# The order of VectorE's queue in a two-layer cross-attention kernel: c and values behind p5, exps, shares and denominators at other stops

## The chip, the cores and the metric

The kernel runs on one core of one Trainium2 chip. The metric is the device time of one execution in microseconds (us); lower is better. A core has five engines with a queue each: TensorE (PE in the profile, its weight loads PEld), VectorE (DVE), ScalarE (ACT), GpSimd (POOL) and SyncE (SP), which here only issues DMAs.

## The reference, cut to what matters

Two cross-attention layers, one behind the other. x is 4 x 512 x 320 (batch, rows, channels), the context 4 x 1024 x 512; 20 heads of 16 channels. The last four context tokens of layer 0 are "image" tokens with weights of their own; in layer 1 the text has 77 tokens and all others are image tokens.

```python
# layer 0
probs_t  = softmax(q @ k_t.T * 0.25)              # 1020 text tokens
text_out = probs_t @ v_t
qsem     = l2norm(probs_t @ text_ehs)             # a 512-wide mix of the raw context, per head
fused    = q @ k_ip.T * 0.25 + 0.5 * (qsem @ ip_n.T)
ip_out   = softmax(fused) * spatial_mask @ v_ip
x        = (text_out + ip_out) @ W_out + b_out + x
# layer 1, on that x
out = (softmax(q @ k.T / 4) @ v + softmax(q @ k_ip.T / 4) @ v_ip) @ Wo.T + bo + x
```

Of qsem only its product with four tokens and its norm are needed. The norm (a sum of squares over 512 columns) makes layer 0 heavy: probs_t times the raw context, for each head.

## The kernel before, in words

**Tiling.** A *turn* is 128 rows of one batch; there are 16. A turn has five *groups* of four heads (80 in all, numbered gi; g is gi modulo 5, turn gi // 5). A group has two *units* (class Unit, i = 0 and 1) of two heads each. The keys lie on partitions, in two halves of four tiles.

**A unit's products.** The matrix product of the two heads' exponentials (four blocks e11, e12, e21, e22; head by half) with the context (two halves of rows, two of columns) is done with seven block products in place of eight, with sums and differences of blocks, as in Strassen's and Winograd's schemes. GpSimd forms the needed combinations of e (L964, L1032, L1051, L1053); sums of the context (t1 to t4) are prepared in DRAM. Text: a product "11·t1" takes block e11 and context block t1. The seven in PE's order, by part:

- part0: b1 = 11·11; ScalarE copies it to p1 (L1050); b2 = 12·21. Then DVE: c = b2 + p1 for the sum of squares of the first head's first half (L1055; ScalarE squares and sums c) and the values of the first head (L1056, 21 columns).
- part1: b3 = 11·t1; DVE copies it to p5 (L1064) and p5's last 21 columns (L1065); then b1 += s2·t2, copied by ScalarE to u (L1068).
- part2: b3 += 12·22, so p5's copy must be done; DVE: c = b3 + u (L1073); b1 += 21·t3; DVE: c = b1 + p5 (L1079, "c of t3").
- part3: b1 += 22·t4, so c of t3 must have been read; ScalarE squares b1, DVE adds the second head's values (L1084).

b1, b2 and b3 are three PSUM banks in rotation. A fourth bank (tp, L105) serves everything else that PE writes in the steady part: transposes of maxima (mx), pt_s, pt_o, pt_y, pt_xT, pt_q, pv and the projections.

**Stops.** After each part comes `stop(gi, k)` (L1262), k = 0 to 3 for the first unit and 4 to 7 for the second. A stop puts one item of other work between the parts:

- scores of the next group in layer 0 (`fill0`, at k = 0 and 2) and of a group of layer 1 (`do_fill`, at k = 4 and 6): 32 short matmuls to `sc`, then per half two maxima on DVE and two copies on ScalarE (L557 to L566);
- folds of these maxima (k = 3, 7, 1), whose transpose on PE (mx) and negated maximum on DVE (zt) follow in part0 or part2; zt goes to DRAM (zd) and comes back broadcast (bc), both issued by SP;
- additions of bc to e, each followed by ScalarE's exp: layer 0's from `ew` (two at k = 6, one at k = 1, one in part2 of the first unit), layer 1's by `do_adds` (one at k = 3, three at k = 5); at k = 6 layer 1's product with its values (pv, 72 instructions);
- items of four lists: `after` and `late` (a finished turn's chain), `norm` (layer 1's denominators, `normalise`, L744: a transpose and a reciprocal on DVE, for even g also a transpose `turn_back`, then two operations on GpSimd, L758 and L759), `proj` (the next batch's projections, while there are any).

**A finished turn's chain.** After a turn's last group `finish` (L1086) runs `norms` at once and queues `exps` (seven small DVE operations, three matmuls pt_s), which queues `shares` (four DVE operations), `turn_out` (transposes pt_o, three copies) and `multiply` (pt_y, an addition to xr); multiply calls `layer1`, which queues x_part (transposes pt_xT), second (pt_q, two writes to q1d) and start (eight loads of layer 1's queries and keys). Layer 1's fifth group brings turn_back and project (pt_y, an addition y, the output's DMA) to the head of `late`.

**What sets the order.** DVE's and PE's instructions are kept in the order in which the program issues them (`vec`, `mm` and `tr`, L77 to L93); DVE instructions thus wait in line behind one that waits. Those of ScalarE, GpSimd and SP are put in order by a planner.

Of the kernel before, what the change touches and what calls it, by code (L numbers as in the profile page):

```python
# [15 lines left out]
ALU = mybir.AluOpType  # L16
# [16 lines left out]
HG = H // 4  # L33
# [12 lines left out]
EH = E // 2  # L46
# [10 lines left out]
def xattn_pair(ctx_stack: ExitStack, tc: tile.TileContext, a: dict, out: bass.AP):  # L57
# [19 lines left out]
    def mm(out, lhsT, rhs, start, stop, on=False):  # L77
        tc.keep_in_program_order(nc.tensor.matmul(out, lhsT=lhsT, rhs=rhs, start=start, stop=stop, skip_group_check=on))  # L78
# [11 lines left out]
    vec = InOrder(nc.vector)  # L90
# [14 lines left out]
    def tp(name):  # L105
        turn_of[0] += 1
        return spare(3 - turn_of[0] % 2 if tail[0] else turn_of[0] % 4 if idle[0] else 3, name)
# [411 lines left out]
    late = deque()  # L519
    proj = deque()  # L520
# [3 lines left out]
    after = deque()  # L524
    ew = deque()
    bits = deque()

    def gap(n=1):
        for _ in range(n):
            if bits:  # L530
                bits.popleft()()
# [74 lines left out]
    class Once:  # L606
# [52 lines left out]
        def ask(self, pt):  # L659

            zd = spread(pt, 8, "zd1", self.name)
            self.bc = bc = big.tile([P, 2, 4, P], F32, tag="bc1", name=f"bc{self.name}")
            keep(nc.sync.dma_start(bc[:NTXT1, 0], zd[0:4, :].partition_broadcast(NTXT1)))
            keep(nc.sync.dma_start(bc[NTXT1:, 0], zd[4:8, :].partition_broadcast(P - NTXT1)))
            keep(nc.sync.dma_start(bc[:, 1], zd[4:8, :].partition_broadcast(P)))
            self.v = load_values(self.z, self.turn, self.g)
# [68 lines left out]
    def do_values():  # L735
        if now["add"] and not now["add"][0].work:
            now["add"].pop(0).values()
# [264 lines left out]
    class Unit:  # L1002
# [43 lines left out]
        def part0(self, between):  # L1046
            self.b1, self.b2 = self.psum(0)[:, 0:WIN], self.psum(1)[:, 0:WIN]
            self.product(self.b1, "11", "11", True)
            self.p1 = big.tile([P, WIN], F32, tag="p1", name=f"p1_{self.name}")
            nc.scalar.copy(self.p1, self.b1)  # L1050
            nc.gpsimd.tensor_tensor(self.e("11"), self.e("11"), self.s2, ALU.add)  # L1051
            self.product(self.b2, "12", "21", True)
            nc.gpsimd.tensor_tensor(self.e("12"), self.e("12"), self.s2, ALU.subtract)  # L1053
            ask = between and between()
            self.add_square(self.b2[:, 0:EH], self.p1[:, 0:EH], 0, 0)  # L1055
            vec.tensor_tensor(self.values(0), self.b2[:, EH:], self.p1[:, EH:], ALU.add)  # L1056
            if ask:
                ask()

        def part1(self):  # L1060
            self.b3 = self.psum(2)[:, 0:WIN]
            self.product(self.b3, "11", "t1", True)
            self.p5 = big.tile([P, WIN], F32, tag="p5", name=f"p5_{self.name}")
            vec.tensor_copy(self.p5[:, 0:EH], self.b3[:, 0:EH])  # L1064
            vec.tensor_tensor(self.p5[:, EH:], self.b3[:, EH:], self.p1[:, EH:], ALU.subtract)  # L1065
            self.product(self.b1[:, 0:EH], "s2", "t2", False)
            self.u = big.tile([P, EH], F32, tag="u", name=f"u_{self.name}")
            nc.scalar.copy(self.u, self.b1[:, 0:EH])  # L1068

        def part2(self, between):  # L1070
            self.product(self.b3[:, 0:EH], "12", "22", False)
            ask = between and between()
            self.add_square(self.b3[:, 0:EH], self.u, 0, 1)  # L1073
            if ask:
                ask()
            if not self.i:
                item(ew)
            self.product(self.b1[:, 0:EH], "21", "t3", False)
            self.add_square(self.b1[:, 0:EH], self.p5[:, 0:EH], 1, 1)  # L1079

        def part3(self):
            self.product(self.b1, "22", "t4", False)
            self.square(self.b1[:, 0:EH], 1, 0)
            vec.tensor_tensor(self.values(1), self.b1[:, EH:], self.p5[:, EH:], ALU.add)  # L1084

    def finish(turn):  # L1086
# [6 lines left out]
        def wide(t, n=NIP):  # L1093
            return t.unsqueeze(2).to_broadcast([P, H, n])
# [30 lines left out]
        def exps():  # L1125
            vec.tensor_tensor(rn, rn, r, ALU.mult)
            vec.tensor_tensor(sem, pv[:, :, D : D + NIP], wide(rn), ALU.mult)
            pt = tp(f"pt_s_{name}")[:, 0 : H * NIP]
            for c in range(NC):
                mm(pt, qt[:, c, :], kd[:, c].rearrange("p h n -> p (h n)"), c == 0, c == NC - 1)  # L1130
            vec.scalar_tensor_tensor(pe, sem, SEM_SCALE, pt.rearrange("p (h n) -> p h n", h=H), ALU.mult, ALU.add)
            vec.tensor_reduce(mx, pe, AX.X, ALU.max)
            vec.tensor_tensor(pe, pe, wide(mx), ALU.subtract)
            nc.scalar.activation(pe, pe, AF.Exp)
            vec.tensor_tensor(o, pv[:, :, 0:D], wide(r, D), ALU.mult)
            gap()
# [31 lines left out]

        def exps_and_on():
            exps()  # L1170
            late.extend([shares, turn_out, multiply])

        (after if turn + 1 < len(TURNS) else late).append(exps_and_on)
# [61 lines left out]
    def item(*queues):  # L1235
        for q in queues:
            if q:
                q.popleft()()
                break

    def visit(gi, k):

        if gi == len(G) - 1:
            if k == 0:
                begin(ep, "e0")
            if k == 4:
                begin(e1p, "e1")
            if k == 6:
                do_values()
                do_adds(2)  # L1250
            do_fill(k // 2 % 2)
            return
        if k < 4:
            fill0(gi + 1, k // 2)
        if k == 4:
            begin(e1p, "e1")
            do_fill(0)
        if k == 6:
            do_values()
            do_fill(1)  # L1260

    def stop(gi, k):  # L1262

        end = gi == len(G) - 1
        if k == 1:
            do_mask() if end else do_rest()
            item(ew)
        if k == 3:
            do_fold(True) if end else fold0(gi + 1)
        if k == 6:  # L1270
            item(ew)
            item(ew)
        if k == 7 and not end:
            do_fold(gi + 1 == len(G) - 1)
        if k == 7 and end and now["fill"]:
            now["fold"] = now["fill"]
            now["fill"] = None
            bits.extend(now["fold"].pieces())
        if k < 3:
            item(after, late, *([proj] if k else []))  # L1280
        elif k % 2:
            item(late, proj)
        do_adds(({3: 4, 7: 2} if end else {3: 1, 5: 3}).get(k, 0))
        if k == 3:
            item(norm)
        if k == 5:
            do_mask()
        if k % 2 == 0:
            visit(gi, k)
        stops[0] += 1  # L1290

    units = {}
# [83 lines left out]
```

## Time and profile before

| | before |
|---|---|
| runs of the kernel, median of 3 | 3320.31 us (3315.03 to 3322.67) |
| the profiled execution | 3314.02 us |
| its span, first to last instruction | 3312.3 us |
| mean granted clock of TensorE | 0.985 |
| steady part, 2127 to 3165 us: busy PE, DVE, ACT, POOL | 1018, 901, 653, 359 of 1038 us |
| last part, 3165 to 3312 us: busy PE, DVE | 117, 86 of 147 us |
| DVE maxima of scores, 128x1024 and 128x768 | 470 x 1222 ns, 150 x 951 ns |
| DVE additions e<-e,bc of 1024 | 470 x 1262 ns |
| a group without projections, turn 13, group 3 | 32.9 us |

A line of a group of instructions reads: line, engine, operation, out<-in, shapes, count, busy time and mean of one, idle time ahead of it and what ended that. A line of waits reads: who waited, for whom, us in total, how often, the longest. A line of the order of time reads: start, duration, instruction, and in brackets idle time ahead with what ended it. All DVE operations of interest have line L88 (a helper), all matmuls L78, so they are told apart by tiles. Consecutive matmuls overlap in the profile: a product of eight matmul instructions takes 1.73 us (256 columns) or 1.87 us (277 columns) from its start to the next one's start, less than the duration shown.

### The profile page before, as it was taken

The page shows a single profiled execution, that of the slowest core. Times are in us where ns is not written, and L with a number is a line of the kernel's source. Part 1 is how long each engine was busy: PE and PEld are TensorE (multiplying, and loading weights), DVE is VectorE, ACT ScalarE, POOL GpSimd, SP SyncE. Part 2 cuts the span into 40 slices and gives each one's busy share as a digit, 9 for nine tenths or more (in the row PEclk, how much of TensorE's full clock was granted, in tenths as well). Part 3 has the DMA queues.
Part 4 walks back from the last instruction along what each step waited for, and adds up shares of the span by engine and source line. Part 5 has one row for each costly group of instructions (what it writes and reads, how often), then busy time and mean ns, then how long its engine had stood idle before and what let it go on. Part 6 is the DMA issues. An engine that isn't in the chain of part 4 may idle for free.

```text
span 3312.3 us, 72573 instructions
## 1 busy us (share of the span) xinstructions
PE 3208.6 (97%) x27740; PEld 2594.7 (78%) x27740; DVE 2506.2 (76%) x4172; ACT 1855.7 (56%) x3373; POOL 1043.7 (32%) x1123
## 2 busy tenths in 40 slices
PE   7999999999999999999999999999999999999988
PEld 5777888878788788887878888887787778787765
DVE  3344577788877777778887787778898888889874
ACT  1333455566555555566655555566666656666643
POOL 3333223323332332323333232323333333333320
PEclk9999999999999999999999999999999999999987
DMA  6433344333444344332344434333233233232221
GB/s 213 112 79 97 96 117 96 92 71 65 102 99 125 92 119 118 75 79 65 68 101 127 121 90 109 97 72 70 58 86 89 63 67 69 59 72 62 64 54 39
DMA packets 648147, 293.89 MB, mean 89 GB/s; under 512 B 491530, under 2 KB 602282, under 8 KB 647802
## 3 DMA queue, kind: packets, MB, share of 16 engines
q1 hardware_dynamic: 646762, 285.65, 36.1%
q8 instruction: 221, 3.62, 0.5%
q0 software_dynamic: 864, 3.41, 0.4%
q14 instruction: 124, 1.02, 0.1%
q10 hardware_dynamic: 176, 0.20, 0.0%
HBM read 248.43 MB, written 40.47 MB: 87 GB/s over the span
## 4 chain that ended last, share of the span: by engine, by line
PE 80%; DVE 10%; DMA 5%; ACT 3%; issue 2%; SPq 1%; POOL 0%; DVEq 0%; POOLq 0%; ACTq 0%
PE b L78 52%; PE sc L78 9%; PE pt_v L78 4%; PE pv L78 4%; PE pt_k L78 4%; DVE e L88 4%; DMA bc<-zd 2%; PE pt_q L78 2%; DVE m L88 2%; PE pt_y L78 2%; DMA zd<-zt 1%; ACT e L561 1%; ACT e L675 1%; DVE x L88 1%; PE mx L78 1%
## 5 line engine op out<-in xcount | busy, mean ns | idle before, releaser
L88 DVE TENSOR_REDUCE m<-sc 128x256 f32<-128x1024 f32 (+1 forms) x620 | 706.9, 1156 | 240.9 <-PE sc L78 166.7
L88 DVE TENSOR_TENSOR e<-e,bc 128x1024 f32<-128x1024 f32 (+2 forms) x770 | 803.5, 1082 | 21.6 <-DMA bc<-zd 21.1
L78 PE MATMUL b<-xv_t,e 128*128 128x277 f32 x2560 | 686.2, 410 | 7.9 <-DVE c L88 7.8
L561 ACT COPY e<-sc 128x1024 f32<-128x1024 f32 x620 | 614.5, 1006 | 82.8 <-DVE m L88 34.2
L78 PE MATMUL b<-xv,e 128*128 128x277 f32 x2560 | 631.3, 398 | 9.2 <-ACT e L962 9.2
L78 PEld LDWEIGHTS b<-xv,e 128*128 128x128 f32 x2560 | 483.4, 190 | 130.6 <-ACT e L962 11.4
L964 POOL TENSOR_TENSOR e<-e 128x512 f32<-128x512 f32 x160 | 230.6, 1441 | 1114.0 <-ACT e L962 1114.0
L78 PEld LDWEIGHTS b<-xv_t,e 128*128 128x128 f32 x2560 | 460.7, 190 | 134.8 <-DVE c L88 11.8
L962 ACT ACTIVATE e<-e 128x1024 f32<-128x1024 f32 x320 | 338.5, 1058 | 225.4 <-DVE e L88 224.6
L675 ACT ACTIVATE e<-e 128x1024 f32<-128x1024 f32 x300 | 316.1, 1058 | 194.3 <-DVE e L88 185.8
L78 PEld LDWEIGHTS sc<-qq,kq 17*128 17x128 f32 (+1 forms) x9920 | 307.1, 186 | 89.9 <-issue 85.0
L78 PE MATMUL sc<-qq,kq 17*128 17x128 f32 (+1 forms) x9920 | 366.8, 283 | 2.1 <-DMA kq<-kd 1.5
L1036 ACT ACTIVATE junk<-c 128x256 f32<-128x256 f32 x480 | 197.6, 412 | 287.8 <-DVE c L88 281.0
L78 PE MATMUL b<-xs,e 128*128 128x256 f32 x1280 | 313.5, 389 | 36.2 <-DVE p L88 27.5
L1051 POOL TENSOR_TENSOR e<-e,s 128x512 f32<-128x512 f32 x160 | 208.4, 1302 | 420.1 <-PE b L78 419.4
L78 PE MATMUL b<-xs_t,e 128*128 128x256 f32 x1280 | 307.3, 384 | 0.0
L78 PEld LDWEIGHTS b<-xs,e 128*128 128x128 f32 x1280 | 241.6, 193 | 81.1 <-issue 47.1
L78 PE MATMUL b<-xs_t,s 128*128 128x256 f32 x1280 | 302.3, 379 | 0.0
L88 DVE TENSOR_TENSOR c<-b,p 128x256 f32<-128x256 f32 x320 | 132.9, 415 | 222.7 <-PE b L78 166.2
L78 PEld LDWEIGHTS b<-xs_t,s 128*128 128x128 f32 x1280 | 242.7, 190 | 39.6
L78 PEld LDWEIGHTS b<-xs_t,e 128*128 128x128 f32 x1280 | 241.8, 194 | 36.9 <-issue 1.0
L1032 POOL TENSOR_TENSOR s<-e,e 128x512 f32<-128x512 f32 x160 | 203.1, 1270 | 122.6 <-ACT e L962 101.5
(213 smaller groups left out, 3439.3 us busy)
## 6 DMA issues: line engine op xcount, KB each, us to landing
kq<-kd SPq DMA_DIRECT2D x632, 64.0 KB
bc<-zd SPq DMA_DIRECT2D x155, 256.0 KB
v1q<-v1d SPq DMA_DIRECT2D x80, 373.5 KB
xv<-v0d SPq DMA_DIRECT2D x320, 42.0 KB
xv_t<-v0d SPq DMA_DIRECT2D x320, 42.0 KB
bc<-zd SPq DMA_DIRECT2D x75, 154.0 KB
L_xattn_W_k<-in_L_xattn_W_k_dram SPq DMA_DIRECT2D x13, 640.0 KB
L_xattn_Wv_ip<-in_L_xattn_Wv_ip_dram SPq DMA_DIRECT2D x13, 640.0 KB
```

The costliest lines, as they stand in the source:

```text
L78: tc.keep_in_program_order(nc.tensor.matmul(out, lhsT=lhsT, rhs=rhs, start=start, stop=stop, skip_group_check=on))
L88: return lambda *args, **kw: keep(getattr(self.engine, name)(*args, **kw))
L561: nc.scalar.copy(e[i].rearrange("p h t s -> p (h t s)"), ps[i].rearrange("p h n -> p (h n)"))
L675: nc.scalar.activation(flat, flat, AF.Exp)
L962: nc.scalar.activation(flat, flat, AF.Exp)
L964: nc.gpsimd.tensor_tensor(e[:, 1], e[:, 1], e[:, 0], ALU.subtract)
L1032: nc.gpsimd.tensor_tensor(self.s2, self.e("21"), self.e("22"), ALU.add)
L1036: nc.scalar.activation(junk, x, AF.Square, accum_out=self.w["ss"][:, self.h + r, k : k + 1])
L1051: nc.gpsimd.tensor_tensor(self.e("11"), self.e("11"), self.s2, ALU.add)
```

## The change

Five edits, all in the order of issue; no instruction is added, removed or resized.

1. c and values of the first products (L1055, L1056) move from part0 to part1, behind p5.
2. c of t3 comes ahead of c = b3 + u, which moves from its place before 21·t3 to the end of part2. The negated maximum zt (`ask`) is no longer behind a c in either part.
3. `after` (the exps) is served at k = 3 in place of k = 0. The list `late` is served at k = 0 to 3, 5 and 7 as before, so the chain behind the exps shifts: turn_out to k = 5, multiply to k = 7, x_part, second and start to k = 0, 1 and 2 of the next group.
4. The shares are served at the end of k = 4 (`brief` tells them).
5. Denominators (`norm`) are served at k = 7, in a turn's first group at k = 3 as before.

```diff
@@ -1052,8 +1053,6 @@
             self.product(self.b2, "12", "21", True)
             nc.gpsimd.tensor_tensor(self.e("12"), self.e("12"), self.s2, ALU.subtract)
             ask = between and between()
-            self.add_square(self.b2[:, 0:EH], self.p1[:, 0:EH], 0, 0)
-            vec.tensor_tensor(self.values(0), self.b2[:, EH:], self.p1[:, EH:], ALU.add)
             if ask:
                 ask()
@@ -1063,6 +1062,8 @@
             vec.tensor_copy(self.p5[:, 0:EH], self.b3[:, 0:EH])
             vec.tensor_tensor(self.p5[:, EH:], self.b3[:, EH:], self.p1[:, EH:], ALU.subtract)
+            self.add_square(self.b2[:, 0:EH], self.p1[:, 0:EH], 0, 0)
+            vec.tensor_tensor(self.values(0), self.b2[:, EH:], self.p1[:, EH:], ALU.add)
             self.product(self.b1[:, 0:EH], "s2", "t2", False)
@@ -1070,13 +1071,13 @@
             ask = between and between()
-            self.add_square(self.b3[:, 0:EH], self.u, 0, 1)
             if ask:
                 ask()
             if not self.i:
                 item(ew)
             self.product(self.b1[:, 0:EH], "21", "t3", False)
             self.add_square(self.b1[:, 0:EH], self.p5[:, 0:EH], 1, 1)
+            self.add_square(self.b3[:, 0:EH], self.u, 0, 1)
@@ -1168,6 +1169,7 @@
             exps()
+            brief.append(shares)
             late.extend([shares, turn_out, multiply])
@@ -1277,16 +1281,18 @@
         if k < 3:
-            item(after, late, *([proj] if k else []))
+            item(late, *([proj] if k else []))
         elif k % 2:
-            item(late, proj)
+            item(*([after] if k == 3 else []), late, proj)
         do_adds(({3: 4, 7: 2} if end else {3: 1, 5: 3}).get(k, 0))
-        if k == 3:
+        if k == (3 if g == 0 else 7):
             item(norm)
         if k == 5:
             do_mask()
         if k % 2 == 0:
             visit(gi, k)
+        if k == 4 and late and late[0] in brief:
+            item(late)
         stops[0] += 1
```

More of the change, by code (lines that the diff above doesn't have):

```diff
@@ L526, in xattn_pair @@
     bits = deque()
+    brief = []
     def gap(n=1):
@@ L1262, in stop @@
     def stop(gi, k):
+        g = gi % HG
         end = gi == len(G) - 1
```

## The prediction

> **What bounds the kernel now.** I read the page's first part, then the waits of TensorE (PE), then the order of time around single waits. The page:
>
> ```profile
> span 3312.3 us, 72573 instructions
> PE 3208.6 (97%) x27740; PEld 2594.7 (78%) x27740; DVE 2506.2 (76%) x4172; ACT 1855.7 (56%) x3373; POOL 1043.7 (32%) x1123
> ```
>
> PE is busy nearly always. The change neither adds nor removes an instruction, so it can only move PE's waits. The waits of PE, largest first:
>
> ```profile
> PE b L78 <- DVE p L88: 27.5, 20, 4.1
> PE b L78 <- ACT e L962: 9.2, 4, 2.8
> PE b L78 <- issue: 8.7, 3, 2.9
> PE b L78 <- DVE c L88: 7.8, 14, 0.6
> ...
> PE pv L78 <- ACT e L675: 4.4, 8, 2.0
> ```
>
> The first is product 12·22, which adds to b3 and has to wait until VectorE (DVE) has copied p5 out of it. Of its 20 waits, 12 (15.2 us) lie in the first unit of a turn's first group, 7 (8.2 us) in second units, one (4.1 us) in the last group. The three of "issue" are the same place at the first group of turns 4, 8 and 12. "DVE c" is product 22·t4 waiting for c of t3, mostly in the same units. So 44.0 us at most are within reach of the change. Why p5 is late, turn 14, first group, in order of time:
>
> ```profile
> 2849.07 0.26 DVE L88 RECIPROCAL r<-pv 128x20 f32<-128x20 f32 x1
> ...
> 2850.69 0.41 DVE L88 TENSOR_TENSOR c<-b,p 128x256 f32<-128x256 f32 x1
> ...
> 2851.30 0.18 DVE L88 TENSOR_TENSOR rn<-rn,r 128x20 f32<-128x20 f32 x1
> ...
> 2852.09 1.89 PE L78 MATMUL b<-xs_t,s 128*128 128x256 f32 x8
> ...
> 2852.97 2.35 DVE L88 TENSOR_REDUCE m<-sc 128x256 f32<-128x1024 f32 x2
> ...
> 2855.24 0.41 DVE L88 COPY p<-b 128x256 f32<-128x256 f32 x1
> ...
> 2855.89 0.89 PE L78 MATMUL b<-xs,e 128*128 128x256 f32 x3 [1.91 <-DVE p L88]
> ```
>
> DVE works without a pause: norms (2849.07 to 2850.69, 1.62), c and values (0.6), exps (2851.30 to 2852.97, 1.67), two maxima (2.27), p5. PE could have begun 12·22 at 2852.09 + 1.73 = 2853.82 and began 2.07 later. A second unit, turn 7, group 1:
>
> ```profile
> 1573.74 1.94 DVE L88 TENSOR_TENSOR e<-e,bc 128x768 f32<-128x768 f32 x1 [0.40 <-DMA bc<-zd]
> 1575.60 0.43 DVE L88 STREAM_TRANSPOSE den<-pc 128x256 f32<-128x256 f32 x1
> ...
> 1576.19 0.39 DVE L88 TENSOR_TENSOR c<-b,p 128x256 f32<-128x256 f32 x1
> ...
> 1578.97 0.41 DVE L88 COPY p<-b 128x256 f32<-128x256 f32 x1
> ```
>
> Denominators (1575.60 to 1576.19, 0.59) and c with values (0.4) stand before a late p5; PE lost 1.1.
>
> **The change, part by part.** Steps are start to start, in us, from turns 13 and 14.
>
> *First groups, first unit (15).* c, values and exps leave the front of p5. The denominators of the group before (0.59) come in at k=7. Also the three pt_s matmuls (2848.29 to 2849.01, 0.72) leave this unit, so PE is ready sooner. Turn 14: after fold_text at 2849.07 come denominators to 2849.66, norms to 2851.28, maxima to 2853.55, p5 and its second part to 2854.05, PE 0.15 later at 2854.20. PE is ready at 2853.82 - 0.72 = 2853.10. A wait of 1.1 stays. I take 1.1 for turns 3, 7, 11, 13, 14, 15 (6.6). Turns 4, 8, 12 by the same count from 1699.45: p5 lets PE go at 1703.73, ready at 1701.68: 2.05 each (6.2). Turns 1, 2, 5, 6, 9, 10 still have projections queued, which now run at k=1 in front of 12·22 (a block of such matmuls is 1 to 3): nothing stays. Removed 15.2 + 8.7 = 23.9, back 12.8.
>
> *c of t3 first.* It starts as 21·t3 ends, 1.1 (the scores' matmuls) ahead of 22·t4; it takes 0.42. The 7.8 go. Behind this c, which waits for PE now as it did, stand only c of b3 and the maxima. c of b3 behind it is hidden by the scores (the maxima wait for PE there anyway: 0.79 at 2792.44 in the steady group).
>
> *Second units (7).* c and values 0.4 and denominators 0.59 to 0.86 leave, more than the 1.1: 8.2 go. In the last group 0.4 + 0.9 of its 4.1 go: 1.3.
>
> *First groups, second unit (15): the price.* k=3 there now has exps (1.67) in place of xr's addition (0.48), k=4 the shares (2858.13 to 2859.14, 1.01), and PE loses its cover, pt_y (2.16), to k=7. From the start M of 22·t4, DVE: maxima 0.2 + 2.28, merge and v1 0.7, fold 1.34, exps 1.67, first addition 1.2, denominators 0.86, zt 0.2, two short maxima 1.82, shares 1.01, p5 0.5 = M + 11.8; PE may start 12·22 at M + 11.9. PE: 22·t4 1.95, pt_s 0.72, two products 3.74, mx 0.11, scores 1.1, 11·t1 1.93, s2·t2 1.73, pt_o 0.5 = M + 11.8. (exps' wait for pt_s adds nothing: PE has it at M + 2.7, DVE asks at M + 5.) So p5 costs 0.1 to 0.2. Behind it come c and values (0.4), the copies of pt_o (0.73) and three additions (3.47) with ScalarE's exp (1.15) before the last fourth of pv's needs: 5.8 after p5, while PE needs it 4.9 after (two products 3.5, then 43 of 72 instructions at 0.029, 1.25, and 0.15). Price 0.9 + 0.2 = 1.1, times 15 = 16.5. Nothing covers this; ends 0 and 2 each.
>
> *Denominators at k=7 elsewhere.* In a steady group the first p5 has 0.7 of slack now (second part done at 2786.69, 12·22 at 2787.46), and c's 0.4 leave the front: 0.59 to 0.86 more fits. GpSimd's two operations (0.40 + 0.32) come after its last `12` subtraction there; cost 0. At the end of group 2 they bring `turn_back` to k=0 and `project` to k=1 of group 3. turn_back then waits about 0.5 for GpSimd, and behind it the maxima and p5, under the 1.6 of cover that pt_y gives in front of 12·22; y's addition (0.48) is late for mx, which needs the same bank: 0.35 times 14 = 4.9, ends 0 and 1 each.
>
> *Layer 1's queries.* x_part, second, start move to k=0, 1, 2 of group 1. second issues two writes of q1d, start eight loads of qq and kq; first use stays at k=4. From pt_q's end to that fill PE has 1.73 + 0.11 + 1.82 + 1.1 + 1.95 + 3.74 + 0.11 = 10.6. Needed: 2886.37 (pt_q's end) to 2892.2 (last qq issue), 5.8, and the landing, 1.5 if it is like zd's in the chain of waits (1.33, 1.69), 5.8 if like bc's. 7.3 fits; with the eight layer-0 loads (3.7) in between on SP's queue it is 11.0, 0.4 late; with bc's landing 1.0 late. I take 0, by zd's row, which is the nearer in size; ends 0 and 1.0 times 15.
>
> *zt before c* lets zd leave 0.35 earlier; bc is waited for 21 us in DVE's rows, hardly on PE's path: 0, ends -3 and 0.
>
> *Behind a long p5 wait* the next products run slow with no releaser (12·22 takes 2.56 at 1522.99 and 3.48 at 1705.47, against 1.89): 10 us in turns 1, 3, 4, 7, 8, 12, 13, never behind the short waits. As these shrink to about half I count half: -5; ends -10 and 0.
>
> [...] Additions e<-e,bc take 1.22, but 2.06 at 2859.67, when GpSimd's subtraction had started at 2859.38. [...]
>
> **Sum:** gains 23.9 + 7.8 + 8.2 + 1.3 + 5 = 46.2; back 12.8 + 16.5 + 4.9 = 34.2; net -12. The profiled execution took 3314.0 (span 3312.3 and 1.7 around it), 6.3 under the median of the runs, inside their spread; so 3302 on its scale and **3308** on the median's.
>
> **Rivals.**
> 1. *The prices don't arise*: GpSimd, SP and ScalarE follow closely, pv and y are in time. Then -46 + 12.8 = -33: 3287. For it: my chain misses its mark by under 1 us everywhere. Against: 14 steps without a gap. Chance 0.20.
> 2. *It only moves the waits*: p5's go, pv's and the first unit's return as large (2 each in place of 1.1, no 5 behind): within 6.6 of 3320. The same holds if the long waits are set by norms alone. Chance 0.20.
> 3. *Slower by GpSimd's order*: den's product and sum are put in front of `e11 += s2` of the next unit. Its order isn't the program's: at 1537.49 they stand between L1051 and L1053, in most groups behind both. rden is ready 3.1 after 11·11 ends; then 0.9 and 1.27 give 5.3, against 11·t1's start 3.0 after: 2.3 per group. From 6 groups on the 12 are gone; in 16 of 64 it is +37 - 12 = +25: 3345; a few groups, or the queries late by 1.0 (+15 - 12), give 3323 to 3334. For it: GpSimd already waits 105.7 us (26 times) for rden. Against: none of that reached PE. Chance 0.22.
> 4. *As forecast*, 3301 to 3313: 0.38.
>
> **How the numbers follow.** 0.2% is 6.6 us, about what a measurement of this kernel can tell from no change. Faster: 0.38 + 0.20 = 0.58; same 0.20; slower 0.22. The range takes rival 1 to just under its time (3283) and leaves out the larger half of rival 3: up to 3335.
>
> **What would show it.** Right: "PE b <- DVE p" falls from 27.5 (and the 8.7) to about 15, "PE b <- DVE c" to nearly nothing, no p5 wait in second units of groups 1 to 4; "PE pv <- ACT e L675" grows from 4.4 to 15 or so; mx waits for DVE y. Wrong: waits of 11·t1 for GpSimd's L1051 (rival 3), of sc for qq (late queries), or p5 waits of 2 that remain.

## The result, and the profile after

The changed kernel takes 3350.93 us, median of 6 runs (3347.94 to 3356.95), beside 3319.77 (3315.03 to 3324.69, 6 runs) of the kernel before on the same chip: a ratio of 1.0096, 95% interval 1.0082 to 1.011. It is slower by 31 us where 12 less were forecast, and lies outside the range. The profiled execution took 3352.46, which is 38.4 more than the one before; the prologue, which the change does not touch, is 3.6 of that.

The first lines of the page after, and TensorE's (PE's) waits (who waited, for whom: us in total, how often, the longest):

```profile
span 3350.8 us, 72578 instructions
...
PE 3227.8 (96%) x27740; PEld 2596.8 (77%) x27740; DVE 2502.4 (75%) x4172; ACT 1860.5 (56%) x3373; POOL 1011.1 (30%) x1123
```

```profile
PE b L78 <- DVE p L88: 27.4, 43, 4.2
PE pt_o L93 <- DVE pe L88: 21.2, 15, 1.8
PE pv L78 <- ACT e L676: 13.8, 24, 1.8
...
PE b L78 <- issue: 3.7, 3, 1.2
...
PE b L78 <- DVE c L88: 3.1, 6, 0.5
...
PE mx L93 <- DVE y L88: 1.8, 7, 0.3
```

The number of matmuls is the same. Of the 38.4, half is in idle time of PE between its records (from 100.3 to 119.5 in all), and half stands as busy time (3208.6 before, 3227.8 here). The latter is mostly pv, whose instructions come piecemeal when its inputs are late: its first 44 take 2.26 at 1782.04, against 1.50 at 1741.23, and no row of waits says so. The rows of waits show only half of the loss. The wait of 12·22 for p5 has not shrunk (27.5, 20 times, before): its long ones are shorter, and there are 23 more. pt_o's wait for the shares is new, pv's has grown by 9. "DVE c" and "issue" have fallen.

**Where the 38 us are.** A unit is measured here from one copy of p1 (ACT, `p<-b`) to the next. In turns 11 to 14, which have no projections, a turn is 3.2 us longer than before; in turns 2 to 10 it is 2.8. In turn 13, as the clearest:

| unit | before | after | what it is |
|---|---|---|---|
| first group, first unit | 22.43 | 16.85 | exps, pt_s, pt_o, pt_y gone from here, p5's wait shorter |
| first group, second unit | 20.15 | 23.35 | shares, pt_o, pt_y come here |
| group 1, first unit | 15.38 | 18.05 | 2.66 of matmuls (pt_xT, pt_q) moved here from the first group |
| group 1, second unit | 17.48 | 18.91 | a loss of 1.4 |
| group 2, second unit | 19.11 | 17.49 | 1.6 of matmuls (pt_y of layer 1) moved away |
| group 3, both units | 32.86 | 36.05 | those 1.6, and a loss of 1.6, most in the second unit |

So in this turn the first group, for which the change was costed, comes out at about nothing (-5.58 + 3.20 + 2.66 = +0.3), and **groups 1 and 3 lose 1.1 to 1.6 us each**, where the forecast had 0 and 0.35.

Turns 2 to 10 are another matter: there projections move from group to group, so lengths of units can't be compared. What can is each of PE's steps, from the start of one matmul to the start of the next, against the usual step (the 20th percentile of both traces) of that matmul. What is above it is lost time, and the change from before to after is:

| lost, us | first group, first unit | first group, second unit | group 1 | group 3 | groups 2 and 4 | sum |
|---|---|---|---|---|---|---|
| turns 2 to 10 | -18.9 | +27.2 | +14.0 | +2.0 | +1.2 | 25.4 |
| turns 11 to 14 | -10.5 | +11.4 | +6.5 | +6.2 | -0.8 | 12.7 |

Groups 1 and 3 hold nearly all of the loss in turns 11 to 14, and 16 of 25 in turns 2 to 10; over all 13 turns they hold 28.6 of 38.1, and the first groups 9.2. Group 3 loses 1.5 a turn in turns 11 to 14 and only 0.2 in turns 2 to 10; most of group 1's loss in turns 4, 5, 8 and 9 is in pv (6.9), not in p5.

**How such a loss looks.** Turn 14, from the first unit of group 3 to product 12·22 of its second, in the order of time: before,

```profile
2965.18 0.33 SPq L584 DMA_DIRECT2D zd<-zt  x1
...
2966.53 0.31 SPq L663 DMA_DIRECT2D bc<-zd  x1
...
2971.36 0.39 ACT L1050 COPY p<-b 128x277 f32<-128x277 f32 x1 [1.13 <-PE b L78]
...
2972.04 1.85 DVE L88 TENSOR_TENSOR e<-e,bc 128x256 f32<-128x256 f32 x2
...
2973.92 1.06 ACT L675 ACTIVATE e<-e 128x1024 f32<-128x1024 f32 x1 [2.17 <-DVE e L88]
...
2977.18 0.41 DVE L88 COPY p<-b 128x256 f32<-128x256 f32 x1
...
2978.04 1.89 PE L78 MATMUL b<-xs,e 128*128 128x256 f32 x8
```

and after:

```profile
3001.24 0.36 SPq L774 DMA_DIRECT2D out_dram<-y  x1
...
3001.65 0.42 SPq L153 DMA_DIRECT2D xr<-in_x_dram  x1
...
3002.17 0.40 SPq L585 DMA_DIRECT2D zd<-zt  x1
...
3004.34 0.30 SPq L664 DMA_DIRECT2D bc<-zd  x1
...
3008.41 0.39 ACT L1051 COPY p<-b 128x277 f32<-128x277 f32 x1 [1.14 <-PE b L78]
...
3010.54 1.87 DVE L88 TENSOR_TENSOR e<-e,bc 128x768 f32<-128x768 f32 x1 [0.47 <-DMA bc<-zd]
...
3012.44 1.06 ACT L676 ACTIVATE e<-e 128x1024 f32<-128x1024 f32 x1 [3.64 <-DVE e L88]
...
3014.43 0.96 DVE L88 TENSOR_REDUCE m<-sc 128x256 f32<-128x768 f32 x1 [0.96 <-ACT e L562]
...
3015.31 0.41 DVE L88 COPY p<-b 128x256 f32<-128x256 f32 x1
...
3015.95 0.45 PE L78 MATMUL b<-xs,e 128*128 128x256 f32 x1 [0.70 <-DVE p L88]
```

Read both from the copy of p1 (2971.36 and 3008.41). Before, zd's write takes 1.35 to the issue of bc, bc is issued 4.83 ahead of the copy, and VectorE's (DVE's) two additions (256 and 768 elements) run without a pause, from +0.68 to +2.53. After, with the output's store and the next rows' load issued in front of zd, the write takes 2.17 and bc is issued 4.07 ahead; the second addition waits 0.47 and then takes 1.87. It ends at +4.00, ScalarE's exp and its copies of the scores follow late, the second maximum waits 0.96 for a copy, p5 comes at +6.90 in place of +5.82, and PE waits.

Why 1.87, when the shape takes 0.95? GpSimd's own order of time in the two second units, before:

```profile
2971.47 1.27 POOL L1051 TENSOR_TENSOR e<-e,s 128x512 f32<-128x512 f32 x1 [2.68 <-PE b L78]
2973.27 1.75 POOL L1053 TENSOR_TENSOR e<-e,s 128x512 f32<-128x512 f32 x1 [0.54 <-PE b L78]
```

and after:

```profile
3008.52 1.27 POOL L1052 TENSOR_TENSOR e<-e,s 128x512 f32<-128x512 f32 x1 [2.14 <-PE b L78]
3010.33 1.27 POOL L1054 TENSOR_TENSOR e<-e,s 128x512 f32<-128x512 f32 x1 [0.54 <-PE b L78]
```

Before, the addition of 768 (the last 0.95 of the row at 2972.04, so from 2972.94) starts first, and GpSimd's subtraction takes 1.75 in place of 1.27. After, GpSimd is 0.21 ahead, and the addition ends 0.81 behind it. Over the whole trace of before, the additions of 768 take 0.95 (129 of 150) when nothing runs on GpSimd at their start, and 1.4 in the middle, up to 2.1, in the other 21; the subtractions of L1053 take 1.27 in the middle (129 of 160) when no addition e<-e,bc runs at their start, and 1.75 in the other 31. So the wait of 0.47 came with 0.92 more for the addition itself, 1.4 together. That GpSimd's earlier start is the cause is the author's reading; no run takes its operation away to try it.

**The margin.** So one number should tell a late second unit from one in time: from bc's first issue to the next copy of p1. All 20 traces of this study, turns 3, 7 and 11 to 14, groups 1 to 4; units longer than 19.1, in which other matmuls lie, are left out:

| margin, us | units | longer than 17.48 by over 0.5 | mean loss |
|---|---|---|---|
| under 4.4 | 78 | 76 | 1.15 |
| 4.4 to 4.75 | 33 | 20 | 0.8 |
| 4.75 to 4.9 | 106 | 13 | 0.2 |
| over 4.9 | 95 | 3 | 0.04 |

It is a step of 1.1 to 1.4 near 4.7, with a blurred edge (20 of 33 are late just below it, 13 of 106 just above). The kernel before stood at 4.83 in most groups, 0.1 above it.

### The profile page after: what moved, and what is told of

It reads as the page before. It is cut to its first block, busy times and chain, and to the rows that moved or that the text cites. A ratio compares the mean times of both kernels' runs of the same rounds, so it can differ in the third digit from the quotient of the medians.

```text
span 3350.8 us, 72578 instructions
## 1 busy us (share of the span) xinstructions
PE 3227.8 (96%) x27740; PEld 2596.8 (77%) x27740; DVE 2502.4 (75%) x4172; ACT 1860.5 (56%) x3373; POOL 1011.1 (30%) x1123
## 4 chain that ended last, share of the span: by engine, by line
PE 57%; DVE 23%; ACT 8%; DMA 7%; issue 3%; SPq 2%; POOL 0%; DVEq 0%; POOLq 0%; ACTq 0%
PE b L78 33%; DVE e L88 9%; PE sc L78 6%; DVE m L88 5%; PE pt_k L78 5%; PE pt_v L78 4%; DMA bc<-zd 4%; ACT e L562 3%; PE pv L78 3%; ACT e L676 2%; PE pt_q L78 2%; DVE x L88 2%; ACT e L963 2%; PE pt_y L78 1%; DMA zd<-zt 1%
## 5 line engine op out<-in xcount | busy, mean ns | idle before, releaser
L965 POOL TENSOR_TENSOR e<-e 128x512 f32<-128x512 f32 x160 | 212.8, 1330 | 1165.9 <-ACT e L963 1165.9
L78 PE MATMUL b<-xs,e 128*128 128x256 f32 x1280 | 313.4, 388 | 31.1 <-DVE p L88 27.4
L1052 POOL TENSOR_TENSOR e<-e,s 128x512 f32<-128x512 f32 x160 | 204.9, 1280 | 336.8 <-PE b L78 335.6
L1054 POOL TENSOR_TENSOR e<-e,s 128x512 f32<-128x512 f32 x160 | 214.7, 1342 | 59.4 <-PE b L78 57.9
```

The source lines that it names most:

```text
L965: nc.gpsimd.tensor_tensor(e[:, 1], e[:, 1], e[:, 0], ALU.subtract)
```

## The experiments

All were timed in five rounds beside the kernel before. Ratios are to that, with the 95% interval. "Late" counts margins under 4.7 among 24 units (turns 3, 7, 11 to 14, groups 1 to 4): 5 before, 15 in the changed kernel.

### Parts of the change: e1 to e4, e9, e13

e1 has edits 1 and 2, e2 edits 3 and 4, e3 edit 5, e4 edits 1, 2 and 5; later e9 edit 1 alone and e13 edit 2 alone. The lines are those of the change's diff, e.g. e13:

```diff
             ask = between and between()
-            self.add_square(self.b3[:, 0:EH], self.u, 0, 1)
             if ask:
...
             self.add_square(self.b1[:, 0:EH], self.p5[:, 0:EH], 1, 1)
+            self.add_square(self.b3[:, 0:EH], self.u, 0, 1)
```

e2 and e3:

```diff
-            item(after, late, *([proj] if k else []))
+            item(late, *([proj] if k else []))
...
-            item(late, proj)
+            item(*([after] if k == 3 else []), late, proj)
...
+        if k == 4 and late and late[0] in brief:
+            item(late)
```

```diff
-        if k == 3:
+        if k == (3 if g == 0 else 7):
             item(norm)
```

> Edits 1 and 2 alone (c and values behind p5, c of t3 first). Theory (the loss comes from the shifted chain of a finished turn): 5 to 20 us faster than before, TensorE's waits for p5 down by some 10 us and for c of t3 from 7.8 to about 3. Rival A (the loss comes from the order inside the unit, because the two squares now come together on ScalarE ahead of its copies of the scores): 10 to 30 us slower.

> Edits 3 and 4 alone (exps at k=3, shares at k=4, the chain behind them later). Theory: 20 to 40 us slower than before, with about 20 us of waits of pt_o for the shares, 10 or more of pv for ScalarE, and p5 late in second units of groups 1 and 3. Rival A: within 10 us of before, because it carries none of the order inside the unit. Rival B (denominators at k=7): within 10 us as well.

> Edit 5 alone (denominators at k=7). Theory: within 7 us of before, faster if anything, since the 0.6 to 0.9 us leave the front of second units. Rival B (the denominators at k=7 delay first units, or GpSimd's sums, or bring project into group 3): 15 to 30 us slower.

> The change without edits 3 and 4. Theory: 5 to 25 us faster than before, since what is left only takes work from the front of p5. Rivals A and B: still 15 us slower or more, about what they give to one of the two left parts.

> The kernel before with the first edit alone (c and values behind p5). Edits 1 and 2 together gave 17 us. Theory (most of it is p5, which is earlier by c's and values' 0.4 to 0.6 wherever it is late; c of t3 first adds only the 4.7 us that PE's wait for c fell by): 10 to 14 faster than before, a ratio of 0.996 to 0.997. Rival (c of t3 and zt ahead of c carry the gain): within 5 of before, 0.9985 to 1.0015.

> The kernel before with the second edit alone (c of t3 ahead of c of b3, both behind 21.t3). Edits 1 and 2 gave 17 us together, the first alone none. Theory (the second carries the gain: zt is no longer behind c, and c of t3 is ready for 22.t4): 12 to 20 faster than before, ratio 0.994 to 0.9965. Rival (neither works without the other: zt needs both c's out of its way, one in part0 and one in part2): 3 to 8 faster, no more than the 4.7 of PE's wait for c.

| kernel | edits | median | ratio | late of 24 | margin in groups 1, 3 (medians) |
|---|---|---|---|---|---|
| before | none | 3315 to 3320 | 1 | 5 | 4.71, 4.82 |
| e1 | 1, 2 | 3299.87 | 0.9948 (0.993 to 0.9966) | 4 | 5.12, 5.11 |
| e9 | 1 | 3319.41 | 1.0007 (0.9994 to 1.002) | 6 | 4.47, 4.79 |
| e13 | 2 | 3293.89 | 0.9928 (0.9917 to 0.994) | 2 | 5.12, 5.11 |
| e3 | 5 | 3335.34 | 1.005 (1.003 to 1.0069) | 21 | 4.72, 4.21 |
| e4 | 1, 2, 5 | 3318.19 | 1.0007 (0.9991 to 1.0022) | 10 | 5.12, 4.28 |
| e2 | 3, 4 | 3382.5 | 1.0208 (1.0183 to 1.0234) | 8 | 3.04, 4.82 |
| change | all | 3350.93 | 1.0096 (1.0082 to 1.011) | 15 | 3.32, 4.14 |

Edits 1 and 2 alone are a gain, so the loss isn't in them. Edit 5, costed at 4.9, costs 17 alone, and takes the 17 of edits 1 and 2 away again (e4, for which neither the theory nor the rivals had "no change"). The chain costs about 30 on top of these and 69 by itself, more than any theory had: there PE also waits 12.7 us (9 times) for layer 1's queries, and a part is the clock. In turns 1 to 14 of e2 the trace grants TensorE half its clock in 24 stretches of 3.4 or 6.8 us (92 us together), against 8 of 3.4 (27 us) before and 4 (14 us) in the changed kernel; 11 of the 24 lie in the first groups' second units, where PE waits for the shares. At half speed those 65 us more are some 32 us of e2's loss (an estimate from these numbers).

And of edits 1 and 2 it is the second that gains: **alone it is the fastest kernel of the study, 24 us faster than before.** Edit 1, which was to make p5 earlier, gives nothing alone. Edit 2 takes c out of zt's front, so that margins rise by 0.3, from 4.83 to 5.12, away from the step; PE's wait for c of t3 falls from 7.8 to 3.1, and "issue" from 8.7 to 6.9:

```profile
PE b L78 <- DVE p L88: 23.6, 16, 4.6
...
PE b L78 <- issue: 6.9, 3, 2.9
...
PE b L78 <- DVE c L88: 3.1, 6, 0.5
```

These waits account for 10 of the 15.4 us between the two profiled executions. The margin gives little of the rest: counted by PE's steps as above, e13 gains 11.7 us in turns 2 to 14, 9.5 of them in the first groups' first units, and only 2.2 in groups 1 to 4, where the margins were counted; the last turn gives 4.8. Whether edit 1 on top of edit 2 costs anything is open: e1 is 6 us slower than e13, but their intervals overlap.

### e5 and e12: the output's chain out of group 3

e5 lets turn_back and project wait until k = 3 and 5 of group 3; e12 is e4 with the denominators back at k = 3 in group 2, so that turn_back and project have their old stops.

```diff
-            item(late, *([proj] if k else []))
+            item(*([] if late and late[0] in outs and gi < len(G) - HG else [late]), *([proj] if k else []))
```

```diff
-        if k == (3 if g == 0 else 7):
+        if k == (3 if g in (0, 2) else 7):
```

> The changed kernel, but a turn's last denominators (turn_back) and its output (project) are not served at k = 0 to 2 of group 3: turn_back runs at k = 3 and project at k = 5, so that the output's DMA and the load of the next rows no longer stand between zd's write and bc's load on SP's queue. Theory (a late bc by SP's queue): the changed kernel loses about 1.5 us in each group 3 of 14 turns, mostly in the second unit; this goes, 15 to 22 us, so 3329 to 3336 against 3351. Rival (the loss is the later y ahead of mx, or GpSimd's denominators beside DVE): the second unit's wait for p5 stays, and the time is within 6 of the changed kernel's.

> Edits 1, 2 and 5 without the chain, but in each turn's group 2 the denominators stay at k = 3, so that turn_back and project keep their old stops (k = 5 and 7) and do not come to the front of group 3. Theory (the fifth edit's 17 us are the output's chain in group 3): 12 to 18 faster than edits 1, 2 and 5 (3318), so 3300 to 3306. Rival (denominators at k = 7 cost by themselves, in the first unit's front, in every group): within 6 of 3318.

e12: 3308.53, ratio 0.9973 (0.9959 to 0.9987), 10 faster than e4: less than expected, but the margin of group 3 is back at 5.10 and its units are as long as before in turns 7 and 11 to 14. So 10 of edit 5's us come from the denominators of group 2 and the output's chain behind them; of the 12.2 between the two profiles in turns 2 to 14, 5.9 lie in group 3. The other 8 or 9, which e12 lacks to e1, lie in the first groups (p5 waits 27.7 against 21.6). e5: 3361.1, ratio 1.0132 (1.0114 to 1.015), a miss: 10 slower, not 20 faster. Group 3's loss falls from 1.6 to 0.9 in turn 13, but zd's round trip in group 4 grows to 1.87, 2.19 and 3.45 in turns 12 to 14, with no issue in between, and group 4 then loses 1.1 to 1.5. Why that write takes so long there is open.

### e6 and e8: VectorE's order inside the changed kernel

e6 serves the shares ahead of the maxima at k = 4; e8 undoes edit 2.

```diff
+        if k == 4 and late and late[0] in brief:
+            item(late)
         if k % 2 == 0:
             visit(gi, k)
-        if k == 4 and late and late[0] in brief:
-            item(late)
```

```diff
             ask = between and between()
+            self.add_square(self.b3[:, 0:EH], self.u, 0, 1)
...
-            self.add_square(self.b3[:, 0:EH], self.u, 0, 1)
```

> The changed kernel with the shares ahead of the maxima at k = 4, where the change puts them behind. Theory (DVE's total work ahead of p5 is what is late, not the order of shares and maxima): the 21.2 us of pt_o's wait for the shares go, but the maxima and zt are later by the shares' 1.0, and a wait of 12.22 for p5, or of the next product behind bc, takes most of it back: 0 to 10 faster than the changed kernel, 3341 to 3351. Rival (PE's stop at pt_o is itself the price): all of the 21 goes, 3330.

> The changed kernel with the second edit undone: c = b3 + u is back ahead of zt in part2, c of t3 stands alone behind 21.t3. Theory (two squares in a row on ScalarE hold up its copies of the scores, and the second maximum waits): the wait of the maxima for ScalarE's copies falls from 126 us to 70 to 90, and where a late p5 follows some of it is gained: 5 to 12 faster than the changed kernel. Rival (zt ahead of c is worth more, since bc is late anyway, and c of t3 ahead saves PE's wait for c): 5 to 15 slower, with PE's wait for DVE's c at 8 or more against 3.1.

e6: 3344.3, ratio 1.008 (1.0063 to 1.0097), 6.6 faster than the change, though the two intervals overlap. pt_o's wait falls from 21.2 to 1.2 and p5's grows from 27.4 to 43.1: 20 us of a wait given back as 16 of another. In the first group's second unit DVE's whole work is late, whatever its order. e8: 3350.7, ratio 1.0107 (1.0089 to 1.0125): neither theory. The maxima's wait for ScalarE's copies falls from 126.3 to 110.7 only, and nothing follows from it; edit 2 is worth nothing here since groups 1 and 3 stay under the step without it as with it (13 late against 15). So nothing here speaks for the crowding of ScalarE's squares as a cause, though the dose was small.

### e7 and e11: what stands between zd and bc

e7 serves `late` only from k = 3 on; e11 has layer 1's first query loads, the output's store and the next rows' load issued by ScalarE.

```diff
-            item(late, *([proj] if k else []))
+            item(*([late] if gi >= len(G) - HG else []), *([proj] if k else []))
```

```diff
-        nc.sync.dma_start(t, a["x"][b, s * P : (s + ns) * P, :].rearrange("(t p) c -> p t c", p=P))
+        (nc.scalar if ns == 1 else nc.sync).dma_start(t, a["x"][b, s * P : (s + ns) * P, :].rearrange("(t p) c -> p t c", p=P))
...
-            nc.sync.dma_start(qq[l][k][32 * r : 32 * r + D, :], q[c : c + D, :])
+            (nc.scalar if l and not g else nc.sync).dma_start(qq[l][k][32 * r : 32 * r + D, :], q[c : c + D, :])
...
-            nc.sync.dma_start(out[b, s * P : (s + 1) * P, :], y)
+            nc.scalar.dma_start(out[b, s * P : (s + 1) * P, :], y)
```

> The changed kernel, but the list late is not served at k = 0 to 2 (in the last turn's groups as before): x_part, second and start come to k = 3, 5 and 7 of group 1, turn_back and project to k = 3 and 5 of group 3. Theory (a late bc by what stands between zd and bc on SP, in groups 1 and 3): both losses go, 1.2 to 1.4 in group 1 and 1.5 in group 3, times 14: 30 to 40 faster than the changed kernel, 3311 to 3321. If then the queries come too late for layer 1's scores at k = 4, a wait of sc for qq takes their place in group 1 or 2 and only group 3's part, about 20, goes. Rival (the losses are VectorE's load alone, whatever SP does): within 8 of the changed kernel.

> The changed kernel, with layer 1's first query loads, the output's store and the next rows' load issued by ScalarE in place of SP, so that SP issues bc as soon as zd has been written. Theory (a late bc by the line on SP): in group 1 the time from zd to bc falls from 2.3 to 2.5 back to about 1.35, and the 1.1 to 1.4 in the second units of group 1 go in up to 15 turns; in group 3 the same if SP's line is the cause there, and nothing if the transfers themselves delay zd: 10 to 35 faster than the changed kernel, 3316 to 3341. Rival (VectorE is late there whatever SP does): zd to bc falls, p5's waits stay, and the time is within 6 of 3351.

e7 begins layer 1 a group later, and leaves out the last of turn 14's five groups of layer 1 with its 128 rows of output, so only its course up to there counts. Its turns 11 to 14, which hold the same 6460 matmuls, take 709.0 us, against 719.9 in the changed kernel and 707.2 before: 11 of the 12.7 us are gone, with 1 late unit of 24 (the whole run: 3324.78, ratio 1.0025, 1.0015 to 1.0035). The two waits:

```profile
PE b L78 <- DVE p L88: 10.5, 22, 3.2
```

```profile
DVE e L88 <- DMA bc<-zd: 8.7, 8, 2.0
```

(33.0 us, 35 times, in the changed kernel for the second). With the chain away from zd the loss of groups 1 and 3 goes: by PE's steps, turns 2 to 14, they are 1.2 us above before in place of 28.6, while the first groups keep their 9.3. (Turns 2 to 10 as a whole keep 13 of their 25 us.) e7 moves operations of DVE and PE along with the DMAs, so it shows where the loss arises, not by which of them. e11 shows that SP's line alone is not it: 3344.41, ratio 1.0083 (1.0065 to 1.0101), 6.5 faster than the change, with overlapping intervals and so neither theory. In group 1, zd to bc falls from 2.48 to between 1.7 and 1.9, but the margin rises to 4.24 only, still under the step, and the second units lose the same 1.10. In group 3 it stays (median of 14 turns 1.89, in the changed kernel 1.88), with neither transfer in SP's line any more, and in e5, where the output comes later, it is 1.34 to 1.39 in turns 11 to 14: that points to the transfers themselves, not the line of issues.

### e10: a smaller shift

Edits 1 and 2, and the exps one stop later, at k = 1.

```diff
-            item(after, late, *([proj] if k else []))
+            item(*([after] if k else []), late, *([proj] if k else []))
```

> Edits 1 and 2, and the exps served at k = 1 in place of k = 0, so behind the first p5 of a turn's first group; the chain behind them shifts by one stop, not by three. Theory (a small shift takes exps' 1.67 out of the first p5's front and leaves shares, pt_o and the queries early enough): 5 to 20 faster than edits 1 and 2 alone (3300): 3280 to 3295, PE's wait for p5 at 10 or less against 21.6. Rival (each shift of the chain costs: it meets the first additions or the query loads meet zd): 3300 to 3320, with waits of pt_o for the shares or more waits of DVE for bc than the 25 or so of before.

3369.69, ratio 1.0151 (1.0127 to 1.0174): 70 slower than e1, a clear miss. p5's wait does fall to 7.8 (6 times), but PE's transposes of the maxima now wait for the chain's operations, 32 us that were not there:

```profile
PE mx L93 <- DVE pT L88: 17.7, 15, 1.2
PE mx L93 <- DVE pe L88: 14.4, 14, 1.6
```

Turns 11 to 14 are only 8 longer than in e1, turns 2 to 10 are 55: at k = 1 the exps take a projection's place, and the displaced projections run later. That this is the cause was not tried. A part is the clock again: half is granted for 55 us of turns 1 to 14, in e1 for 24. Only 6 units are late; the margin is not the whole price of the chain.

### e14 to e18: the suspected causes by themselves

In group 2 of the kernel before, which has no chain: e14 one load, e15 three stores at k = 1; e16 the same stores at k = 3; e17 two stores of c that become ready just before zt; e18 two copies by DVE before zt.

```diff
+        if k == 1 and gi % HG == 2 and gi + 1 < len(G):
+            for n in range(NO):
+                extra = dr.tile([P, C], F32, tag=f"extra{n}", name=f"extra{n}_{gi}")
+                keep(nc.sync.dma_start(extra, wo1[:, n, :]))
```

```diff
             self.add_square(self.b3[:, 0:EH], self.u, 0, 1)
+            if self.i == 0 and self.gi % HG == 2:
+                for n in range(2):
+                    extra = dr.tile([P, EH], F32, tag=f"extra{n}", name=f"extra{n}_{self.gi}")
+                    keep(nc.sync.dma_start(extra, self.c))
             if ask:
```

```diff
+            if self.i == 0 and self.gi % HG == 2:
+                extra = big.tile([P, EH], F32, tag="extra", name=f"extra_{self.gi}")
+                for n in range(2):
+                    vec.tensor_copy(extra, self.b3[:, 0:EH])
             if ask:
```

> The kernel before, with one more load of 160 KB (rows of x, into a tile that nobody reads) issued at k = 1 of each turn's group 2, in front of zd. Theory (transfers ahead of zd hold up the scores' maxima's round trip, and with it the first additions and p5): zd to bc in group 2 grows from 1.35 to 1.7 or more, and a part of the 1.1 per group comes: 4 to 16 us slower than before. Rival (VectorE's and ScalarE's order, not the transfers): within 4 of before.

> The kernel before, with three more stores of 160 KB (the output weights, to DRAM that nobody reads) issued at k = 1 of each turn's group 2, in front of zd. Theory (transfers ahead of zd): zd to bc in group 2 grows to 2.2 or more, and second units of group 2 lose 1 to 2: 15 to 32 us slower than before. Rival (VectorE's and ScalarE's order): zd to bc grows, and the time stays within 5 of before.

> The same three stores issued at k = 3 of group 2, so behind bc's loads on the queue. Theory (it is the place ahead of zd that costs, not the traffic as such): within 5 of before, zd to bc of the first unit at 1.35. Rival (any such traffic in the group slows the loads that are due): 10 us slower or more, as much as with the stores in front.

> The kernel before, with two more stores of 131 KB (c = b3 + u, to DRAM that nobody reads) that become ready just before zt in the first unit of each turn's group 2, so that SP issues them right in front of zd. Theory (a transfer right in front of zd delays it, bc lands late, and the second unit's first addition, the copies of the scores and p5 behind it): zd to bc in group 2 grows from 1.35 to 2.0 or more, and the second units of group 2 lose 0.5 to 1.4: 6 to 20 us slower than before. Rival (VectorE's order in the changed group, not the transfers): zd to bc grows, the time stays within 5 of before.

> The kernel before, with two more copies of 256 elements by VectorE (0.8 us in all, into a tile that nobody reads) ahead of zt in the first unit of each turn's group 2, and no transfer. Theory (what counts is when bc lands, whatever made it late): zd is 0.8 later, and the second units of group 2 lose about as much as by a round trip that is 0.8 longer: 6 to 16 us slower than before. Rival (a zt that is late by 0.8 is within the slack; only the traffic costs): within 5 of before.

e14, e15 and e16 measure 0.9998, 0.9998 and 1.0001 (each within 0.0012): no change. e14 and e15 did not give the dose: in turn 14 of e15 SP had issued the last store 2.7 us ahead of zd, and the round trip stayed at 1.33 to 1.41 in turns 13 and 14 of all three. What they show is that this traffic, early enough or behind bc, cost nothing. e17 does: 3326.39, ratio 1.0034 (1.0022 to 1.0046), 9 us slower. Turn 14:

```profile
2938.22 0.81 SPq L1078 DMA_DIRECT2D extra<-c  x2
...
2939.13 0.40 SPq L584 DMA_DIRECT2D zd<-zt  x1
...
2940.61 0.30 SPq L663 DMA_DIRECT2D bc<-zd  x1
...
2944.58 0.39 ACT L1051 COPY p<-b 128x277 f32<-128x277 f32 x1 [1.13 <-PE b L78]
...
2946.66 1.93 DVE L88 TENSOR_TENSOR e<-e,bc 128x768 f32<-128x768 f32 x1 [0.41 <-DMA bc<-zd]
...
2952.67 1.53 PE L78 MATMUL b<-xs,e 128*128 128x256 f32 x6 [1.24 <-DVE p L88]
```

zd is 0.72 later (SP issues the stores for 0.8), the margin is 3.97, the addition waits 0.41 and takes 1.93, and PE loses 1.24: the changed kernel's group 3, made in a group without the change. The forecast of how was wrong: zd to bc is 1.48, not 2.0 or more, so it is zd's own lateness that makes bc late here. Late units in group 2 lose 1.2 to 1.5 (turns 3, 7, 11, 13, 14), p5's wait rises to 39.1 (29 times). e18 can't tell: 1.0009 (0.9999 to 1.0019). Its copies also made the first unit 1.0 longer in most of these turns (PE waited for c of t3), so that the margin did not shrink (5.05), and the second units lost nothing. That fits the margin, but doesn't try it.

## Why the prediction was wrong, by its own steps

The losses are those of the table above, turns 2 to 14 of the two profiled executions.

- **Mis-sized, and the largest: the first groups' second unit, "price 0.9 + 0.2 = 1.1, times 15 = 16.5".** It lost 38.6 in 13 turns, 3.0 each. pv's part was right (0.88 in turn 14 for 0.9). p5's "0.1 to 0.2" was not: PE waits 1.34 in pt_o for the shares, since the maximum ahead of them waits for a copy of the scores and exps' last subtraction took 1.01 with a GpSimd operation under way (0.24 in turn 14 of before, with none). The count had DVE working without a pause. e6 shows that the order of shares and maxima matters little (6.6 of it, within the noise).
- **Failed: "Layer 1's queries ... I take 0".** Group 1 lost 20.4. The queries themselves were in time, as the count said. But their four loads, and q1d's writes ahead of them, stand by zd: zd to bc 2.48 in place of 1.35, and 1.1 and more lost behind a late bc.
- **Failed: "y's addition is late for mx ... 0.35 times 14 = 4.9".** That wait is there (1.8 us, 7 times). The step counted project's DVE and PE operations and put its two DMAs, right in front of zd, at nothing: bc comes 0.7 later against the copy of p1, and the second unit loses 1.1 more in each of turns 11 to 14. Group 3 lost 8.1 in all.
- **Failed: second units, "8.2 go".** p5 was to be earlier by what leaves its front. PE waits for p5 23 times (21.3 us) in second units of groups 1 to 4, against 8 times (12.4) before, mostly where bc is late.
- **Mis-sized: edit 2, with 7.8 for c of t3 and 0 for zt.** Alone it is worth 24 us (15 between the profiled executions), mostly in first groups. This error went the other way and doesn't explain the slowdown. But "bc is waited for 21 us in DVE's rows, hardly on PE's path" hid that bc was only 0.1 above the step.
- **Right:** the first units (-29.4 in 13 turns, where the terms give about -24 for 15; 0.72 of wait left in turn 14, 1.1 forecast; "issue" 8.7 to 3.7); c of t3 (7.8 to 3.1); pv and y where they were looked for.
- **Right in size, its cause unseen: "Behind a long p5 wait the next products run slow with no releaser".** What is slow is the clock. In the first groups' first units of just these turns (1, 3, 4, 7, 8, 12, 13) the trace of before grants 0.50 of the clock for 3.4 us, at 725.5 us for instance, 0.4 us after a p5 wait of 1.91; at half speed that is 1.7 us each (an estimate from these numbers). None of the seven is left after the change. The same wait of 1.91 in turns 11 and 14 has no such stretch, so what decides it is open.
- **Rivals.** GpSimd's order (3), the case kept for "slower", did not happen: PE never waits for L1052. The result was slower by a way that no rival had. Rival 2 ("only moves the waits") comes near for the first groups. The prediction's row of an addition that took 2.06 beside GpSimd's subtraction has no term in the sum; in the changed kernel's trace above such an addition takes 0.92 more, behind a wait of 0.47.

That a bc made late by DMAs in front of zd costs a unit 1.2 to 1.5 is shown by e17, and that groups 1 and 3 lose their 28.6 by the chain's new place is shown by e7. How much of it is SP's line, the transfers or the moved operations of DVE and PE is not separated. Open are also zd's long round trips in e5.

## What to carry to other kernels

Where a small result goes through DRAM and back in every iteration, measure its margin, from the issue of the load to the point of first use, before anything is moved near it: this kernel, whose margins stood 0.1 us above the step, paid 9 us for DMAs put right ahead of it (e17), and nothing for those that were early enough or behind it (e14 to e16). Count a moved step's DMAs by the neighbours that they get on the queue, not by their own landing. And a wait of an engine that "has time" wasn't free where another engine's operation started first: DVE's wait of 0.47 came with an addition of 1.87 in place of 0.95. Compare PE's busy time and granted clock as well as its rows of waits: here half of the loss stood as busy time.

## What the runs showed of the hardware

- zd's write of 4 KB to DRAM was seen as done (bc issued) 1.33 to 1.40 us after its issue in 18 of 20 groups (turns 11 to 14 before), 2.02 to 2.17 right behind a store and a load of 160 KB (group 3 of the same turns after), and 1.87, 2.19 and 3.45 with no issue in between (e5, turns 12 to 14, group 4).
- SP took 0.30 to 0.59 us for an issue (5th to 95th percentile of 3065 before). With four query loads issued between zd and bc, bc came 2.48 after zd in place of 1.35 (turn 14, group 1), and 1.7 to 1.9 after it with these loads on ScalarE's queue (e11).
- bc, 512 KB in three loads, is there 5.4 to 6.6 us after its last issue, by the 133 additions of 768 that wait for it in turns 11 to 14 of the 20 traces. e11 issued it earlier against the same unit, and it was there no earlier (6.05 in place of 5.39, turn 14, group 1).
- An addition e<-e,bc of 768 elements took 0.95 with nothing on GpSimd at its start (129 of 150 before), and 1.87 and 1.93 where a GpSimd operation had started 0.2 ahead of it (turn 14, after and e17); GpSimd's own operation took 1.75 in place of 1.27 where the addition was ahead (before, 2973.27).
- The granted clock of TensorE was 0.50 in stretches of 3.4 us (some twice as long): 8 in turns 1 to 14 before, 4 after, 24 in e2. Eight matmuls of 256 columns that met one took 2.56, 3.37 and 3.48 us (turns 7, 3 and 8 of before) in place of 1.89.
